# Rotated queries and new keys turned by VectorE blocks and a round trip through DRAM, instead of TensorE transposes

## The chip, the cores and the metric

The kernel runs on one NeuronCore of a Trainium2 chip. The metric is the device time of one execution in microseconds; several runs are taken and their median counts. Five engines work beside each other, each in the order in which its instructions were written out: TensorE (PE in the profile; its weight loads are shown as PEld), VectorE (DVE), ScalarE (ACT), GpSimd (POOL) and SyncE (SP, which here only issues DMAs). Where an instruction needs another engine's result it waits, and all that stands behind it on its own engine waits with it. DMAs are issued from SP's or GpSimd's queue and run on 16 DMA engines.

## The reference, cut to what matters

Four layers with residual sums work on `x` of 64 batches x 32 tokens x 512 channels, all in fp32. Layers 0 and 3 multiply by a 32x32 matrix chosen per batch, layer 1 is a linear layer with a low-rank adapter chosen per batch. Layer 2, where most of the time goes, is attention over a paged cache:

```python
q = jnp.einsum('bsd,ed->bse', x, Wq).reshape(bsz, seqlen, HQ, D)   # 32 heads of 128
k = ...Wk...reshape(bsz, seqlen, HK, D)                            # 8 heads
v = ...Wv...
q = _rope(_rmsnorm(q, q_norm_w), pos)
k = _rope(_rmsnorm(k, k_norm_w), pos)
k_all = concatenate([kc, k], axis=1)     # 512 cached keys by block_table, 32 new ones
scores = jnp.einsum('bqhd,bkhd->bhqk', q, k_all) * SCALE
probs = softmax(where(valid, scores, -1e30))
o = jnp.einsum('bhqk,bkhd->bqhd', probs, v_all)
return jnp.einsum('bse,de->bsd', o.reshape(bsz, seqlen, HQ * D), Wo)
```

`_rope` multiplies the normed vector by cosines, multiplies a copy with its halves swapped by sines, and adds the two. The part that concerns us is what happens to `q` and the new `k` between `_rope` and the scores: the projections leave them with tokens on the partitions, and the scores need them with the 128 head channels on the partitions.

## The kernel before, in words

Tokens are taken in 16 tiles of 128 (four batches of 32). Key heads come in two groups of four (`KG = 4`), and each key head serves four query heads (`REP = 4`). A *step* is one tile with one group, so there are 32 steps; two steps with the same group make a *pair* (16 pairs), whose projections share work in Strassen's manner. A *unit* is one batch in one group: four units a step, 128 in all. A *slot* is one key head of one unit, so there are 512 slots, and the loop `slot(i)` writes out, slot by slot, what every engine does; negative slots are the start, in which layer 1 runs and the first pair is projected. What is done in a slot beside the attention is entered in a plan by slot number (`at(slot, where, ...)`), and `where` ("fetch", "pool", "pe", "take", "late", "power", "turn", "dve", "keep", "act", "store") gives the place in the slot.

In slot i, TensorE computes the scores of head k of its unit (L848 and L851, against 544 keys in one two-bank tile `s_ps`, of which there is one), transposes the probabilities of slot i-2 (`flip`, L890) and multiplies those of slot i-3 by the values (L900). VectorE adds the mask and takes the maximum (L856), copies the turned probabilities out of PSUM (L892) and takes reciprocals; ScalarE does the exponential (L867) and the division (L873, L874). GpSimd gathers a chunk of cached values (L105, one a slot), makes the next unit's mask `pen` (L819, one a unit) and issues some DMAs. SP loads each unit's 16 pages of keys into `kT` (L804) with page numbers read from a table, two units' buffers in turn: unit u's are issued in slot 4(u-1).

Between these lies the next pair's projection, placed so that it ends three slots before the pair's first scores (`AHEAD = 1`): blocks KV, 0 and 1 of `begin_block`, each with seven products (`project`, L664) whose sums VectorE takes into `raw` (L676). A block of queries covers eight heads of both tiles, which come out as four sets of four heads; KV gives the new values, which are stored, and one set of four keys a tile. A `Norm` then handles one set of four heads, 512 elements a partition: ScalarE's squares (L720), GpSimd's power -1/2 (L725, L727), and on VectorE `scale` (L732), `straight` (L739), `swapped` in two halves (L751) and `sum` (L761). `norm_piece` puts these four pieces into slots in order, first come first served, where VectorE's count of pieces in the slot is under two (three in each fourth slot). After the sum, `turn` (L766) has TensorE transpose the four heads into PSUM, and `keep` (L778) has ScalarE copy them to `qT` or `kT_new`. ScalarE copies a unit's new keys beside its cached pages (`begin`, L835), and `scores` reads `qT` from its own tile.

Output tiles `oT` go to DRAM by `store` (L940), half of them on SP's queue and half on GpSimd's, until the last three steps. After the last slot comes the output projection (L1351) and layer 3.

Of the kernel before, what the change touches and what calls it, by code (L numbers as in the profile page):

```python
# [43 lines left out]
P = 128  # L44
# [4 lines left out]
D = 128  # L49
# [28 lines left out]
def resid_kernel(  # L78
# [139 lines left out]

    o_dram = [
# [7 lines left out]
    with ExitStack() as l2:  # L227
# [6 lines left out]
        front_pool = l2.enter_context(tc.tile_pool(name="front", bufs=1))  # L234
# [135 lines left out]
        def rotary(t):  # L370


            if t < 2:
                step = pair_of[0].steps[t]
                step.rot = {kind: rotary_tile(kind, t) for kind in "qk"}
            else:
                rot = start_pool.tile([P, 2, 2, D], F32, name="rot", bufs=2)
                rot_of[t] = {"q": rot[:, 0], "k": rot[:, 1]}
# [11 lines left out]
        def rotary_tile(kind, i):  # L390
            return proj_pool.tile([P, 2, D], F32, name=f"rot_{kind}{i}")
# [177 lines left out]
        class Step:  # L569


            def __init__(self, s):
                self.g, self.t = steps[s]
                self.qT, self.rot = {}, {}

        class Pair:
# [24 lines left out]
            def load_rotary(self, kind):  # L601
                for i, step in enumerate(self.steps):
                    step.rot[kind] = rotary_tile(kind, i)
# [35 lines left out]
        class Block:  # L639
# [17 lines left out]
            def project(self, i, c):  # L657
                x, half, w = self.ORDER[i]
                if c == 0 and i % 2 and self.slots[2 * i] in range(-11, -2):
# [12 lines left out]
            def new(self):  # L672
                return proj_pool.tile([P, REP, D], F32, name="raw", bufs=6)
# [6 lines left out]
            def take(self, i, norm):  # L680

                if i == 0:
                    self.u = self.new()
                    nc.scalar.copy(self.u, self.ps.rearrange("p (h d) -> p h d", h=REP))
                elif i == 1:
                    norm.raw = self.new()
                    self.add(norm.raw, self.u)
                elif i == 2:
                    self.add(self.u, self.u)
                elif i == 3:  # L690
                    self.v = self.new()
                    self.add(self.v, self.u)
                elif i == 4:
                    norm.raw = self.new()
                    self.add(norm.raw, self.v)
                elif i == 5:
                    self.add(self.v, self.v)
                    norm.raw = self.v
                    self.add(self.u, self.u)
                else:  # L700
                    self.add(self.u, self.u)
                    norm.raw = self.u

            def store_values(self, norm, i):
                step = self.pair.steps[i]
                nc.sync.dma_start(
                    out=vn_dram[step.g][step.t], in_=norm.raw.rearrange("p h d -> p (h d)")
                )

        class Norm:  # L710


            def __init__(self, pair, i, k=None):
                self.i, self.step, self.k = i, pair_of[pair].steps[i], k

            def squares(self):
                self.ss = small.tile([P, REP], F32, name="ss")
                sq = proj_pool.tile([P, D], F32, name="sq")
                for h in range(REP):
                    nc.scalar.activation(  # L720
                        sq, self.raw[:, h, :], AF.Square, accum_out=self.ss[:, h : h + 1]
                    )

            def power(self):
                nc.gpsimd.tensor_scalar(self.ss, self.ss, D * EPS, None, ALU.add)  # L725
                self.rstd = small.tile([P, REP], F32, name="rstd")
                nc.gpsimd.tensor_tensor(  # L727
                    self.rstd, self.ss, minus_half.to_broadcast([P, REP]), ALU.pow
                )

            def scale(self):
                nc.vector.tensor_tensor(  # L732
                    self.raw, self.raw, self.rstd.unsqueeze(2).to_broadcast([P, REP, D]), ALU.mult
                )

            def straight(self):
                kind = "k" if self.k is None else "q"
                self.a = proj_pool.tile([P, REP, D], F32, name="rot_a", bufs=2)
                nc.vector.tensor_tensor(  # L739
                    self.a,  # L740
                    self.raw,
                    self.step.rot[kind][:, 0, :].unsqueeze(1).to_broadcast([P, REP, D]),
                    ALU.mult,
                )

            def swapped(self):
                kind = "k" if self.k is None else "q"
                self.b = proj_pool.tile([P, REP, D], F32, name="rot_b")
                half = D // 2
                for i in (0, 1):  # L750
                    nc.vector.tensor_tensor(  # L751
                        self.b[:, :, i * half : (i + 1) * half],
                        self.raw[:, :, (1 - i) * half : (2 - i) * half],
                        self.step.rot[kind][:, 1, i * half : (i + 1) * half]
                        .unsqueeze(1)
                        .to_broadcast([P, REP, half]),
# [3 lines left out]
            def sum(self):  # L760
                nc.vector.tensor_tensor(self.a, self.a, self.b, ALU.add)  # L761

            def turn(self):
                self.tp = ps_t.tile([P, REP, P], F32, name="head_ps", tag="t")
                for h in range(REP):
                    nc.tensor.transpose(self.tp[:, h, :], self.a[:, h, :], ident)  # L766

            def keep(self):

                if self.k is None:  # L770
                    dst = front_pool.tile([P, NB, KG, S], F32, name="kT_new", bufs=3)
                    self.step.kT_new = dst
                else:
                    dst = front_pool.tile(
                        [P, NB, REP, S], F32, name=f"qT_{self.i}", bufs=(4, 6)[self.i]
                    )
                    self.step.qT[self.k] = dst
                nc.scalar.copy(  # L778
                    dst.rearrange("p j h s -> p h j s"),
                    self.tp.rearrange("p h (j s) -> p h j s", j=NB),  # L780
                )

        class Unit:


            def __init__(self, u):
# [6 lines left out]
                self.kT = room["kT"].tile([P, NPP + 1, KG, PSIZE], F32, name="kT")  # L793
# [38 lines left out]

            def begin(self):

                nc.scalar.copy(  # L835
                    self.kT[:, NPP].rearrange("p k s -> p (k s)"),
# [690 lines left out]
```

## Time and profile before

| | us |
|---|---|
| median of 3 runs (2440.8 to 2450.85) | 2444.19 |
| the profiled execution | 2442.28 |
| its span | 2440.4 |
| PE busy in the span | 2401.3 |
| DVE / ACT / POOL busy | 1658.7 / 1397.4 / 1163.8 |
| first scores start | 183.4 |
| DMA: MB moved, mean share of 16 engines | 459.18, 62.7% |

In a row of a group, the shape is followed by the count, then the busy time of the group in us and the mean length of one in ns, then the time its engine was idle before it and who ended that. PE's lengths overlap, since matmuls are pipelined: for what a group costs TensorE, the distance between starts counts. A row of the stretches has, after its window and length, each engine's busy time and count, the clock granted to TensorE as a share, the DMA engines' mean busy share and the rate in GB/s. In a row of a queue's time line, the start and the time from the first issue to the end of the last one come first. SP's rows of waits have the total, the number and the longest.

### The profile page before, as it was taken

What the parts mean: (1) busy time and instruction counts of PE and PEld (TensorE: products, weight loads), DVE (VectorE), ACT (ScalarE), POOL (GpSimd) and SP (SyncE); (2) the same over time, 40 slices, a digit from 0 to 9 for tenths busy, and PEclk for the clock granted to TensorE, in tenths of its full rate; (3) what the DMA queues carried; (4) which work ended last, traced back from release to release, by engine and by line L of the source; (5) the groups of instructions that cost most, each with busy time, mean ns of one, the idle gap of its engine ahead of it and who ended that gap; (6) DMA issues with size and microseconds to landing.
All of it is one profiled execution on the core that took longest, in us unless ns stands there. A gap on an engine that the chain in (4) does not pass through costs nothing.

```text
span 2440.4 us, 47152 instructions
## 1 busy us (share of the span) xinstructions
PE 2401.3 (98%) x13792; PEld 1866.5 (76%) x13792; DVE 1658.7 (68%) x3611; ACT 1397.4 (57%) x4005; POOL 1163.8 (48%) x1146
## 2 busy tenths in 40 slices
PE   7999999999999999999999999999999999999999
PEld 4557777777777777777777777777777788888887
DVE  5667778777777777787777777777777856333222
ACT  2246767777777777777777777777676754000000
POOL 3336555555555556655655555655555653000000
PEclk9999999999999999999999999999999999999999
DMA  8877666666767677866666666666667874333221
GB/s 270 281 241 204 192 195 197 191 204 189 208 186 212 185 218 231 248 189 199 176 190 178 193 171 195 176 189 179 192 183 225 258 242 157 107 117 123 87 91 57
DMA packets 458320, 459.18 MB, mean 188 GB/s; under 512 B 53008, under 2 KB 381072, under 8 KB 454480
## 3 DMA queue, kind: packets, MB, share of 16 engines
q1 hardware_dynamic: 402560, 276.03, 37.4%
q0 software_dynamic: 54928, 179.09, 24.7%
q8 instruction: 111, 1.82, 0.3%
q14 instruction: 145, 1.19, 0.2%
q10 hardware_dynamic: 576, 1.05, 0.1%
HBM read 384.66 MB, written 79.69 MB: 190 GB/s over the span
## 4 chain that ended last, share of the span: by engine, by line
PE 91%; DMA 3%; DVE 2%; issue 1%; ACT 1%; SPq 1%; POOL 0%; ACTq 0%; DVEq 0%; POOLq 0%
PE proj_ps L664 23%; PE o_ps L900 17%; PE out_ps L1351 15%; PE s_ps L848 10%; PE pT_ps L890 9%; PE s_ps L851 8%; PE head_ps L766 3%; PE l_ps L490 2%; PE o_ps L913 1%; DMA o<-oT 1%; DMA kT<-kT 1%; PE s_ps L883 1%; SPq L804 1%; PE mix_ps L1369 1%; DMA rot<-rot 1%
## 5 line engine op out<-in xcount | busy, mean ns | idle before, releaser
L105 POOL DMA_INDIRECT v_sb<-v,v_rows x512 | 544.9, 1064 | 364.1 <-PE o_ps L900 253.6
L900 PE MATMUL o_ps<-pT,v_sb 128*128 128x128 f32 x4096 | 624.0, 275 | 0.0
L900 PEld LDWEIGHTS o_ps<-pT,v_sb 128*128 128x128 f32 x4096 | 578.4, 191 | 27.2 <-DVE pT L892 0.5
L867 ACT ACTIVATE sm<-sm,top 128x544 f32<-128x544 f32 x512 | 380.9, 744 | 345.2 <-DVE top L856 340.7
L856 DVE CUSTOM_DVE_ANT_0 sm<-s_ps,pen 128x544 f32<-128x544 f32 x512 | 369.1, 721 | 114.5 <-PE s_ps L851 110.0
L873 ACT ACTIVATE sm<-sm,share 128x512 f32<-128x512 f32 x512 | 369.9, 722 | 101.0 <-DVE share L872 88.5
L892 DVE COPY pT<-pT_ps 128x512 f32<-128x512 f32 x512 | 353.0, 689 | 56.9 <-PE pT_ps L890 17.7
L848 PE MATMUL s_ps<-kT,qT 128*128 128x288 f32 x1024 | 334.4, 408 | 1.4 <-DMA kT<-kT 1.1
L890 PE MATMUL pT_ps<-ident,sm 128*128 128x128 f32 x2048 | 310.2, 274 | 4.2 <-ACT qT L778 2.7
L851 PE MATMUL s_ps<-kT,qT 128*128 128x256 f32 x1024 | 305.8, 380 | 4.2 <-issue 4.2
L676 DVE TENSOR_TENSOR raw<-proj_ps,raw 128x512 f32<-128x512 f32 x332 | 224.1, 687 | 121.2 <-PE proj_ps L664 121.1
L848 PEld LDWEIGHTS s_ps<-kT,qT 128*128 128x128 f32 x1024 | 179.4, 190 | 148.4 <-issue 126.9
L819 POOL TENSOR_SCALAR pen<-key_f,seq_f 128x544 f32<-128x544 f32 x128 | 284.1, 2220 | 12.9 <-DMA kT<-kT 1.6
L890 PEld LDWEIGHTS pT_ps<-ident,sm 128*128 128x128 f32 x2048 | 239.0, 141 | 8.4 <-ACT qT L778 4.4
L720 ACT ACTIVATE sq<-raw 128x128 f32<-128x128 f32 x640 | 198.5, 310 | 77.3 <-DVE raw L676 61.9
L851 PEld LDWEIGHTS s_ps<-kT,qT 128*128 128x128 f32 x1024 | 194.8, 190 | 58.7 <-issue 5.1
L105 POOL DMA_INDIRECT mix_rows<-in_w,cond_rows x32 | 36.8, 1149 | 353.3 <-DVE mix_diag L170 301.1
L725 POOL TENSOR_SCALAR ss<-ss 128x4 f32<-128x4 f32 x160 | 38.8, 243 | 348.0 <-ACT sq L720 344.4
L872 DVE RECIPROCAL share<-total 128x1 f32<-128x1 f32 x512 | 83.8, 164 | 177.0 <-ACT sm L867 162.8
L1401 ACT COPY p<-out_ps 128x256 f32<-128x256 f32 x7 | 2.6, 372 | 333.1 <-PE out_ps L1351 333.1
L664 PE MATMUL proj_ps<-sum,x 128*128 128x512 f32 x380 | 188.1, 597 | 0.4 <-DVE raw L676 0.4
L727 POOL TENSOR_TENSOR rstd<-ss,minus_half 128x4 f32<-128x4 f32 x160 | 167.6, 1047 | 13.3
(176 smaller groups left out, 3517.2 us busy)
## 6 DMA issues: line engine op xcount, KB each, us to landing
kT<-kT SPq DMA_DIRECT2D x2048, 64.0 KB
o_in<-o SPq DMA_DIRECT2D x28, 1024.0 KB
o<-oT POOLq DMA_DIRECT2D x69, 256.0 KB
o<-oT SPq DMA_DIRECT2D x58, 256.0 KB
page_rows<-in_kv_cache SPq DMA_DIRECT2D x32, 256.0 KB
v<-in_kv_cache SPq DMA_DIRECT2D x32, 256.0 KB
kT<-page_rows SPq DMA_DIRECT2D x32, 256.0 KB
vn<-raw SPq DMA_DIRECT2D x32, 256.0 KB
```

The costliest lines, as they stand in the source:

```text
L105: nc.gpsimd.indirect_dma_start(out=dst, out_offset=None, in_=table, in_offset=bass.IndirectOffsetOnAxis(ap=index, axis=0),)
L664: nc.tensor.matmul(self.ps, lhsT=self.pair.x[x][:, c if x == "b" else half.start + c, :], rhs=blocks(self.b)[w][:, c, :], start=(c == 0), ...
L819: nc.gpsimd.tensor_scalar(self.pen, key_f, seq_f[:, self.b : self.b + 1], BIG, ALU.is_ge, ALU.mult)
L848: nc.tensor.matmul(ps[:, first:HID], lhsT=q, rhs=self.kT[:, :n1, k, :], start=True, stop=True)
L851: nc.tensor.matmul(ps[:, HID : first + LA], lhsT=q, rhs=self.kT[:, n1:, k, :], start=True, stop=True)
L856: nc.vector.tensor_tensor_reduce(out=sm, in0=ps[:, first : first + LA], in1=self.pen, scale=1.0, scalar=3e38, op0=ALU.add, op1=ALU.min, ac ...
L867: nc.scalar.activation(sm, sm, AF.Exp, bias=top, scale=-1.0, accum_out=total)
L873: nc.scalar.activation(sm[:, :L], sm[:, :L], AF.Copy, scale=share)
L890: nc.tensor.transpose(ps[:, c, :], self.sm[k][:, c * P : (c + 1) * P], ident)
L892: nc.vector.tensor_copy(pT, ps)
L900: nc.tensor.matmul(o_of[self.s, k][:, self.j, :], lhsT=self.v[c][:, k * D : (k + 1) * D], rhs=self.pT[k][:, c, :], start=(self.j == 0 and ...
L1351: nc.tensor.matmul(ps[:, :HALF], lhsT=o[:, i, :], rhs=w[i // REP][:, i % REP, :], start=(i == 0), stop=(i == KG * REP - 1),)
```

## The change

The TensorE transposes of the heads and ScalarE's copies of them go. Norms are merged into doubles: one `Norm` now handles eight heads (both tiles' keys, or a tile's two sets of query heads in a block), 1024 elements a partition, so there are 80 instead of 160. Their sum moves from VectorE to GpSimd, one slot after `swapped`. Two slots after `swapped` at the earliest, VectorE turns the eight heads in blocks of 32x32 in one instruction, which puts, for each batch, 32 channels on the batch's 32 partitions. SP stores the result to a DRAM tile `qk` (one store for a tile's queries of a block, two for the keys; 16 x 6 = 96 stores of 256 or 512 KB), and for each unit GpSimd loads its new keys and its four heads of queries into the end of the unit's `kT` buffer, four slots ahead of its scores, with one DMA of 320 KB (128 of them), whose access pattern puts the 4 x 32 channels on 128 partitions. `scores` reads the queries from there.

With that, the projection starts eight slots earlier (`AHEAD = 9`, and the start of the kernel has eight slots more); `kT` has three buffers, each longer by four rows, and a unit's page loads are issued in slot 4(u-2)+1; the planner counts VectorE's pieces in microseconds up to `ROOM`; all output stores go to GpSimd's queue, and `oT` has four buffers instead of three. In the start, more of the projections' sums use the scores' PSUM tile.

```diff
+    qk_dram = [
+        [dram.tile([P, NC, (1 + KG) * P], F32, name=f"qk_{g}_{t}") for t in range(NT)]
+        for g in range(NG)
+    ]
...
             def scale(self):
+                raw = self.raw.rearrange("p i h d -> p (i h) d")
                 nc.vector.tensor_tensor(
-                    self.raw, self.raw, self.rstd.unsqueeze(2).to_broadcast([P, REP, D]), ALU.mult
-                )
+                    raw, raw, self.rstd.unsqueeze(2).to_broadcast([P, 2 * REP, D]), ALU.mult
+                )
...
             def sum(self):
-                nc.vector.tensor_tensor(self.a, self.a, self.b, ALU.add)
+                a, b = [x.rearrange("p i h d -> p (i h d)") for x in (self.a, self.b)]
+                nc.gpsimd.tensor_tensor(a, a, b, ALU.add)
 
             def turn(self):
-                self.tp = ps_t.tile([P, REP, P], F32, name="head_ps", tag="t")
-                for h in range(REP):
-                    nc.tensor.transpose(self.tp[:, h, :], self.a[:, h, :], ident)
-
-            def keep(self):
...
-                nc.scalar.copy(
-                    dst.rearrange("p j h s -> p h j s"),
-                    self.tp.rearrange("p h (j s) -> p h j s", j=NB),
-                )
+
+                self.turned = self.raw.rearrange("p i h d -> p (i h d)").rearrange(
+                    "p (c m s) -> p c m s", c=NC, s=S
+                )
+                nc.vector.transpose(
+                    self.turned, self.a.rearrange("p i h (c e) -> p c (i h) e", c=NC)
+                )
+
+            def store(self):
+                pair = self.block.pair
+                for i in (0, 1) if self.i == KV else (self.i,):
+                    step = pair.steps[i]
+                    if self.i == KV:
+                        heads, first, n = slice(i * REP, (i + 1) * REP), 0, P
+                    else:
+                        heads, first, n = slice(0, 2 * REP), (1 + 2 * self.block.b) * P, 2 * P
+                    nc.sync.dma_start(
+                        out=qk_dram[step.g][step.t][:, :, first : first + n],
+                        in_=self.turned[:, :, heads, :].rearrange("p c m s -> p c (m s)"),
+                    )
...
-                self.kT = room["kT"].tile([P, NPP + 1, KG, PSIZE], F32, name="kT")
+                self.kT = room["kT"].tile([P, NPP + 1 + KG, KG, PSIZE], F32, name="kT")
...
+            def fetch_heads(self):
+
+                nc.gpsimd.dma_start(
+                    out=self.kT[:, NPP:].rearrange("d n k s -> d (n k s)"),
+                    in_=qk_dram[self.g][self.t][self.j * S : (self.j + 1) * S].rearrange(
+                        "e c f -> c e f"
+                    ),
+                )
+
             def begin(self):
 
-                nc.scalar.copy(
-                    self.kT[:, NPP].rearrange("p k s -> p (k s)"),
-                    step_of[self.s].kT_new[:, self.j].rearrange("p k s -> p (k s)"),
-                )
...
-                q = step_of[self.s].qT[k][:, self.j].rearrange("p h s -> p (h s)")
+                q = self.kT[:, NPP + 1 + k].rearrange("p h s -> p (h s)")
...
-            queue = nc.sync if k < 2 and s < len(steps) - 3 else nc.gpsimd
-            queue.dma_start(
+            nc.gpsimd.dma_start(
...
+        ROOM = 2.0
+        COST = {"scale": 1.2, "straight": 1.2, "swapped": 1.3, "turn": 1.2}
+        NEXT = {"scale": "straight", "straight": "swapped", "swapped": "turn"}
...
+            for piece in pieces:
+                ready, norm, name = piece
+                if ready <= slot and busy.get(slot, 0) + COST[name] <= ROOM:
+                    break
+            else:
                 return
...
+            if name == "turn":
+                pieces.pop(at_piece)
+                at(slot + 1, "fetch", norm.store)
+                return
+            later = name == "swapped"
+            if later:
+                at(slot + 1, "take", norm.sum)
+            pieces[at_piece] = (slot + 2 * later, norm, NEXT[name])
...
-        AHEAD = 1
+        AHEAD = 9
...
-            at(KG * (u - 1) if u > 1 else ready + 3 * u, "fetch", make, unit_of, u, Unit, u)
+            at(KG * (u - 2) + 1 if u > 2 else ready + 3 * u, "fetch", make, unit_of, u, Unit, u)
...
+            at(KG * u - (4 if u else 3), "fetch", call, unit_of, u, "fetch_heads")
...
-                    room["kT"] = l2.enter_context(tc.tile_pool(name="kT", bufs=2))
+                    room["kT"] = l2.enter_context(tc.tile_pool(name="kT", bufs=3))
```

## The prediction

> **What bounds the kernel now.** I read the page first (engine shares, then the chain), then a table of stretches, then the groups by shape, then SP's queue. The profiled execution took 2442.28 us, 2440.4 of them span; it stands 1.9 under the median of the three runs, 2444.19, so a sum made on it is a sum on the median within 0.1%. A change under 0.5% (12 us) can't be told from none.
>
> ```profile
> PE 2401.3 (98%) x13792; PEld 1866.5 (76%) x13792; DVE 1658.7 (68%) x3611; ACT 1397.4 (57%) x4005; POOL 1163.8 (48%) x1146
> ...
> PE 91%; DMA 3%; DVE 2%; issue 1%; ACT 1%; SPq 1%; POOL 0%; ACTq 0%; DVEq 0%; POOLq 0%
> ```
>
> TensorE is the path. The stretches (PE, PEld, DVE, ACT, POOL busy; clock; DMA share; GB/s) say where nothing else ends a wait:
>
> ```profile
> 150.00:183.00 33.00, 30.04 (x116) 15.95 (x114) 21.95 (x44) 13.40 (x47) 10.21 (x16) 1.00 0.76 241
> ...
> 240.00:1900.00 1660.00, 1657.88 (x10093) 1274.85 (x10092) 1271.21 (x2825) 1200.75 (x3487) 961.35 (x924) 1.00 0.67 196
> ...
> 900.00:1000.00 100.00, 99.75 (x588) 76.50 (x587) 75.64 (x167) 72.07 (x213) 63.65 (x64) 1.00 0.81 247
> ...
> 1950.00:2000.00 50.00, 44.96 (x306) 39.80 (x305) 28.27 (x64) 28.46 (x69) 28.39 (x30) 0.97 0.78 248
> ```
>
> From 240 to 1900 us TensorE idles 2.1 us in all, so every microsecond of its work removed there is one off the end, until another queue takes over. One pair of steps (32 slots) takes 117.5 us there, and of these VectorE is busy 1271.21/1660 x 117.5 = 90.0, ScalarE 85.0, GpSimd 68.0.
>
> The removed turns in TensorE's order: four transposes of a head group start at 1011.87 and the scores start at 1012.31.
>
> ```profile
> 1011.87 0.60 PE L766 MATMUL head_ps<-ident,rot_a 128*128 128x128 f32 x4
> 1012.31 0.65 PE L848 MATMUL s_ps<-kT,qT 128*128 128x288 f32 x2
> ```
>
> So a group costs 0.44 us of TensorE, start to start, not the 0.60 that its pipelined ends show.
>
> **What goes.** 160 groups (640 transposes) x 0.44 = 70.4 us of TensorE: 10 groups, 4.4 us, a pair, so 117.5 becomes 113.1. With up to 0.45 a group it would be 72 at most; I take 70. ScalarE loses the copies out of these (160 x 0.57) and the key copies (128 x 0.293), 8.0 us a pair: 85 becomes 77. It was not the path; priced at 0.
>
> **VectorE**, per pair, from these rows:
>
> ```profile
> L761 DVE TENSOR_TENSOR rot_a<-rot_a,rot_b 128x512 f32<-128x512 f32 x160 | 119.8, 749 | 2.6
> ...
> L751 DVE TENSOR_TENSOR rot_b<-raw,rot_q 128x256 f32<-128x256 f32 x256 | 101.4, 437 | 0.0
> ...
> L628 DVE TENSOR_TENSOR sum<-wq,sum 128x1024 f32<-128x1024 f32 x8 | 9.7, 1212 | 0.0
> ```
>
> Ten sums go (-7.5). Scale and straight become 5 + 5 of 1024 elements at 1.21 for 10 + 10 of 512 at 0.69 (-1.7); swapped, 10 of 512 at 0.69 for 20 of 256 at 0.43 (-1.7). Five block transposes of 1024 come; the trace has none. Bounds: two PSUM copies of 512 at 0.689 (1.4) less nothing, and twice a 1024-element operation (2.4); I take 1.21, the row of equal size: +6.1. VectorE goes from 90.0 to 85 (91 at the upper end) of 113.1: it keeps over 20 us, and a slot's scores leave it about 1.5 us of lag (3.1 us slot less 0.9 of scores and 0.7 of maximum). Price 0; without that cover each transpose's excess would count, 75 x 1.2 = 90 us.
>
> **GpSimd.** Ten pairs of power operations (0.243 + 1.047) become five of 8 elements (pow 1.05 if fixed, 2.1 if by element): -12.9, +6.5 to 11.7. Eight head loads and four more output stores at 0.594 a direct issue (1.064 if they cost what a gather does) add 7.1 to 12.8. That makes 69 to 80, plus five sums X of 1024 elements. X is the unknown. Below: the same sum on VectorE, 2 x 0.68 = 1.4. Nearest row on the engine:
>
> ```profile
> L819 POOL TENSOR_SCALAR pen<-key_f,seq_f 128x544 f32<-128x544 f32 x128 | 284.1, 2220 | 12.9 <-DMA kT<-kT 1.6
> ...
> L727 POOL TENSOR_TENSOR rstd<-ss,minus_half 128x4 f32<-128x4 f32 x160 | 167.6, 1047 | 13.3
> ```
>
> 2.22 x 1024/544 = 4.2, twice that for two inputs, 8.4. I take 4.2 (same engine, streaming): 90 to 101 of 113, so it stays off the path. Its waits: a sum waits for VectorE's swapped, and the next value gathers queue behind it; the turn, two slots after swapped, waits for the sum. Two slots are 6.5 us and more, so at 4.2 neither is late. I add 2 us in all (0 to 30).
>
> Does the sum slow VectorE? A sum on VectorE that began while the mask ran on GpSimd took 1.10 instead of 0.67 us, and was not held until the mask's end at 1535.51:
>
> ```profile
> 1533.55 1.10 DVE L761 TENSOR_TENSOR rot_a<-rot_a,rot_b 128x512 f32<-128x512 f32 x1
> ...
> 1533.41 2.10 POOL L819 TENSOR_SCALAR pen<-key_f,seq_f 128x544 f32<-128x544 f32 x1
> ```
>
> At 0.43 more for each of 80 sums that is 34 us of VectorE beside TensorE, priced at 0. [...]
>
> **DMA.** Stores of 16 x 2.62 MB and loads of 128 x 0.328 MB are 83.9 MB on 459.18. At the page's own price (62.7% of the span for 459.18 MB) the loop's 0.67 becomes 0.67 x 117.5/113.1 + 0.12 = 0.81 to 0.82. The stretch 900:1000 ran at 0.81 and TensorE lost 0.25 us of 100. Price 0 to 10, inside the next term.
>
> **SP, and what waits behind it.** One pair period of SP from 563.25: eight groups of page loads and what lies between. Some of it:
>
> ```profile
> 563.25 10.18 SPq L804 DMA_DIRECT2D kT<-kT  x16
> 573.52 0.38 SPq L706 DMA_DIRECT2D vn<-raw  x1
> 573.95 0.58 SPq L826 DMA_DIRECT2D v_new<-vn  x1
> ...
> 575.29 0.55 SPq L292 DMA_DIRECT2D kT<-page_rows  x1
> ...
> 606.35 1.09 SPq L940 DMA_DIRECT2D o<-oT  x2
> ```
>
> The eight groups sum to 80.2, the others to 14, register loads of 0.6 to 1.1 before a group make about 7: 101 of 117.5. After: less 1.9 for the output stores, plus six stores at about 0.6: 103 of 113.1. SP is the fullest queue after TensorE. Each store waits for its turn on VectorE, with the next unit's page loads behind it; the head load waits on GpSimd for the store, with value gathers behind it; TensorE needs both. The last turn that a pair's first step needs comes 7 slots ahead of its scores, with a group of 16 page loads (10 us, 3 slots) between turn and store; then store and load, for which the chain lists landings of 2.2 (values) to 6.2 us (output). 10 + 2 x 4 + 1 of issues fits in 7 x 3.5 = 24.5 us with 5 over. Three kT buffers (two before) let SP start page loads 7 slots ahead instead of 4, a relief that can gain no more than the loop's 2.1 us of idle time. Late by 0 to 3 us a pair: 0 to 45 us, I take 12.
>
> **The ends.** Start: unit 0's queries must go through turn, store and load before the first scores. From the last squares that is about 2 + 2 + 4 (VectorE) + 4 (sum) + 1.2 + 4 + 4 = 21 us; the next pair's key and value projections, moved ahead by 8 slots, cover 14 x 0.86 = 12. Before, TensorE already lost 3.0 of 33 us there. +0 to 9, I take 4. Tail: the last 12 slots before the early products have no projection, where 4 had none. They last 2.3 us each, 9.4 a unit against SP's 11 to 12; three units lose 6 us less SP's lead. +0 to 10, I take 4; the stretch 1950:2000 shows the same loss of 5.
>
> **Sum**: 2442.3 - 70 + 2 + 12 + 4 + 4 = 2394; I state 2392, since the first term may be 72.
>
> **Rivals.**
> (a) SP sets the pace: slower. For: its rows of waits, in four periods (400 to 870 us):
>
> ```profile
> SPq L940 <- ACT oT L932: 27.0, 8, 4.7
> SPq L804 <- PE s_ps L851: 25.8, 17, 3.3
> ```
>
> A store that SP reaches before its data costs it 3.4 us. Five turns a pair at that price are 17 us: 103 + 17 = 120 a pair, 2.5 over 117.5, so 15 x 2.5 + 8 for the ends: 2490. It decides from 14.5 us of waits a pair. Against: with three buffers a late SP stops waiting, and the old output waits are gone.
> (b) GpSimd sets the pace: from X = (113.1 - 69)/5 = 8.8, or 6.6 with its dearer rows; no gain left from X = 7.5 to 9.7. At 8.4 with the middle of 74: 116 a pair, 2442 - 70 + 15 x 2.9 + 10 = 2426. Against: 8.4 takes both the mask's rate and a doubling.
> (c) Half the gain: head loads late by 3 us every pair, both ends at their bounds: 2442 - 70 + 45 + 19 = 2436.
> (d) Hidden anyway: it would need VectorE or ScalarE near 117 of 117.5; they have 90 and 85. All costs at 0 gives 2370.
>
> **How the numbers follow.** The forecast (2370 to 2412) 0.62; still better, under 2368, 0.03; (c) and (b) as priced, 2412 to 2456, 0.17, two thirds of it under 2432; (a), or (b) beyond its bound, above 2456, 0.18. Range 2368 to 2456 leaves 0.03 and 0.18 outside; the likeliest case's own is 2370 to 2412. Faster 0.77, same 0.05, slower 0.18.
>
> **What would show it.** A pair period of about 113 us and PE still over 99% busy from 240 to 1880; block transposes near 1.2 us; sums on GpSimd at 2 to 4.5; value gathers on GpSimd not waiting for head loads. Wrong if SP shows hardly a gap, if scores wait for kT, or values for gathers, by several us a pair.

## The result, and the profile after

The changed kernel takes 2791.26 us, the median of four runs (2783.17 to 2795.01), against 2442.86 for the kernel before beside it: a ratio of 1.1415, with a 95% interval of 1.1376 to 1.1454. The forecast was 2392, in a range of 2368 to 2456. The change makes the kernel 14% slower, and the profiled execution (2783.17, span 2781.3) is one of those four. The page, first busy times and then the shares of the chain of waits:

```profile
PE 2422.4 (87%) x13152; PEld 1849.2 (66%) x13152; DVE 1610.6 (58%) x3211; ACT 1300.2 (47%) x3717; POOL 1435.4 (52%) x1252
...
PE 51%; DMA 17%; issue 12%; SPq 8%; DVE 5%; ACT 4%; POOL 4%; POOLq 0%; DVEq 0%; ACTq 0%
```

TensorE had 98% of the span and 91% of the chain; it has 87% and 51%, and 25% of the chain is now DMA or SP's queue. The loop as one stretch (columns as before: PE, PEld, DVE, ACT, POOL busy; clock; DMA share; GB/s):

```profile
300.00:2250.00 1950.00, 1672.64 (x9519) 1259.20 (x9518) 1231.05 (x2485) 1115.75 (x3227) 1210.31 (x1033) 0.94 0.75 208
```

TensorE is idle for 277 of 1950 us, where before it was idle for 2 of 1660. Two things are missing that one would look for in a kernel 14% slower: no other engine is full (the next is VectorE, 63%), and the DMA engines are busier by only 0.08 of their time. Where the time went, with TensorE's busy and idle time added up in three parts of the span (us; "pairs" is the mean of the first fourteen, from the starts of their first scores):

| | before | after | difference |
|---|---|---|---|
| first scores at (TensorE idle until then) | 183.4 (21.8) | 217.5 (46.5) | +34.1 (+24.7) |
| first to last scores | 1862.1 | 2169.0 | +306.9 |
| of it TensorE idle | 12.0 | 307.1 | +295.1 |
| of it TensorE busy | 1850.2 | 1861.9 | +11.7 |
| last scores to the end | 394.8 | 394.9 | +0.1 |
| a pair | 117.3 | 136.7 | +19.4 |

So nearly all of the 341 us is idle time of TensorE in the loop, some 20 us a pair, plus a later start. TensorE's busy time did not shrink although 640 transposes are gone; the reason stands in the next view, five stretches of 5 us around one of the stalls:

```profile
600.00:605.00 5.00, 5.00 (x30) 3.73 (x28) 1.26 (x4) 1.93 (x5) 0.00 (x0) 1.00 0.40 117
605.00:610.00 5.00, 0.03 (x1) 0.00 (x0) 0.00 (x0) 0.00 (x0) 0.00 (x0) 1.00 0.47 148
610.00:615.00 5.00, 0.00 (x0) 0.00 (x0) 0.00 (x0) 0.00 (x0) 0.75 (x1) 0.51 0.58 183
615.00:620.00 5.00, 0.00 (x0) 0.00 (x0) 1.40 (x2) 0.00 (x0) 4.53 (x4) 0.50 0.71 151
620.00:625.00 5.00, 4.53 (x16) 3.09 (x17) 2.57 (x7) 3.36 (x13) 4.43 (x4) 0.63 0.88 206
```

All four engines stand still together for ten microseconds, and the granted clock, 1.00 before the stall, is down to 0.50 in 615 to 620 and 0.63 where TensorE starts again. A later kernel below with the same matmuls and a mean clock of 0.995 (g4_all) has 1957.3 us of busy TensorE up to the last scores, where this one, at 0.945 in the mean, has 170.9 + 1861.9 = 2032.8; some 75 us go with the lower clock.

The time line of that stall, with the idle time before an instruction and its releaser in brackets:

```profile
585.33 8.89 SPq L827 DMA_DIRECT2D kT<-kT  x9
...
586.15 1.23 DVE L789 STREAM_TRANSPOSE raw<-rot_a 128x1024 f32<-128x1024 f32 x1
...
598.60 9.38 SPq L827 DMA_DIRECT2D kT<-kT  x16
...
609.15 0.58 SPq L801 DMA_DIRECT2D qk<-raw  x1
...
614.14 0.75 POOL L858 DMA_DIRECT2D kT<-qk  x1 [23.93 <-DMA kT<-kT]
615.20 1.00 POOL L105 DMA_INDIRECT v_sb<-v,v_rows  x1 [0.31 <-issue]
616.22 2.34 POOL L782 TENSOR_TENSOR rot_a<-rot_a,rot_b 128x1024 f32<-128x1024 f32 x1
618.60 1.25 DVE L789 STREAM_TRANSPOSE raw<-rot_a 128x1024 f32<-128x1024 f32 x1 [17.12 <-POOL rot_a L782]
...
620.47 2.08 PE L672 MATMUL proj_ps<-wk,x 128*128 128x512 f32 x2 [15.44 <-DVE raw L684]
```

Read it downwards. VectorE turns a set of heads at 586. SP gets to the store of it only at 609, 23 us later, because it is still busy with page loads; it does not wait for the turn. The head load on GpSimd waits 23.93 us for that store. Behind the head load on GpSimd stand a value gather and the sum of another norm; behind the sum, on VectorE, a transpose; behind the transpose the additions of the projections; and for those waits TensorE. (The releaser printed at the head load, a page load, is only the landing that came last in the trace.) GpSimd reaches this head load 2.8 us after the turn's end (587.38) and then stands for 23.93 us. Such a wait comes once a pair, fourteen times between 300 and 2250 us, for 15.2 to 25.4 us. SP's own waits, full span, before and after:

```profile
SPq L804 <- DMA kT<-kT: 9.7, 16, 1.9
```

```profile
SPq L827 <- DMA kT<-kT: 259.9, 201, 4.3
...
SPq L607 <- DMA kT<-kT: 34.0, 13, 4.0
SPq L801 <- DMA kT<-kT: 31.7, 21, 4.5
SPq L827 <- DMA qk<-raw: 31.2, 18, 5.4
...
SPq L801 <- DVE raw L789: 8.3, 1, 8.3
```

In the trace SP's DMAs take turns on eight semaphores (336 or 337 on each), and by the rows above a DMA waits there until the eighth before it has landed. Before, all rows of this kind came to 13 us between 300 and 1900 us. Now they are some 358 us between 300 and 2250, 25 a pair. The last row is the wait that the prediction had feared, of a store for its turn: 8.3 us, once.

The landings themselves are longer. From each issue to the last of its semaphore counts, median and ninetieth percentile between 300 and 1900 us: page loads 2.65 and 3.90 before, 4.27 and 8.65 after; value gathers 4.30 and 5.54 before, 5.89 and 9.15 after; the new head loads 9.06 and 10.21. A page load issued 0.6 us before the head load of 614.14 landed in 1.7 us, one issued 0.8 us after it took 7.6. So the theory to test (A): the head load itself is slow, and slows all that is in flight with it. The trace's DMA packets say how. A head load is 64 packets of 5120 bytes; between 300 and 1900 us of the kernel after, at most five of them run at once for over 99% of the time (3.3 in the mean), and from the first to the last of a load 5.8 us pass. That four of the 16 DMA engines carry a load is the author's estimate from these packets; the trace does not number the engines. The load's pattern is "e c f -> c e f": the slowest dimension is `c`, which has four values.

### The profile page after: what moved, and what is told of

The parts are those of the page before. It is cut to its first block, busy times and chain, and to the rows that moved or that the text cites. A ratio compares the mean times of both kernels' runs of the same rounds, so it can differ in the third digit from the quotient of the medians.

```text
span 2781.3 us, 45999 instructions
## 1 busy us (share of the span) xinstructions
PE 2422.4 (87%) x13152; PEld 1849.2 (66%) x13152; DVE 1610.6 (58%) x3211; ACT 1300.2 (47%) x3717; POOL 1435.4 (52%) x1252
## 4 chain that ended last, share of the span: by engine, by line
PE 51%; DMA 17%; issue 12%; SPq 8%; DVE 5%; ACT 4%; POOL 4%; POOLq 0%; DVEq 0%; ACTq 0%
PE out_ps L1386 13%; PE proj_ps L672 12%; PE o_ps L928 8%; DMA kT<-kT 8%; PE s_ps L876 5%; SPq L827 5%; PE s_ps L879 4%; DMA v_sb<-v,v_rows 4%; PE pT_ps L918 4%; ACT sq L731 2%; POOL rot_a L782 2%; PE l_ps L498 2%; ACT sm L895 2%; SPq L819 2%; DVE raw L684 1%
## 5 line engine op out<-in xcount | busy, mean ns | idle before, releaser
L928 PE MATMUL o_ps<-pT,v_sb 128*128 128x128 f32 x4096 | 645.6, 280 | 82.6 <-DMA v_sb<-v,v_rows 82.3
L928 PEld LDWEIGHTS o_ps<-pT,v_sb 128*128 128x128 f32 x4096 | 594.1, 195 | 120.8 <-DMA v_sb<-v,v_rows 91.7
L876 PE MATMUL s_ps<-kT 128*128 128x288 f32 x1024 | 349.4, 424 | 54.8 <-DMA kT<-kT 18.1
L876 PEld LDWEIGHTS s_ps<-kT 128*128 128x128 f32 x1024 | 195.7, 198 | 291.3 <-issue 179.7
L879 PE MATMUL s_ps<-kT 128*128 128x256 f32 x1024 | 315.6, 391 | 8.6 <-DMA kT<-kT 6.4
L858 POOL DMA_DIRECT2D kT<-qk x128 | 98.5, 770 | 327.8 <-issue 193.5
L918 PEld LDWEIGHTS pT_ps<-ident,sm 128*128 128x128 f32 x2048 | 246.4, 144 | 2.0 <-ACT page_rows L286 1.9
L879 PEld LDWEIGHTS s_ps<-kT 128*128 128x128 f32 x1024 | 200.9, 197 | 70.4 <-issue 11.3
L789 DVE STREAM_TRANSPOSE raw<-rot_a 128x1024 f32<-128x1024 f32 x80 | 98.6, 1233 | 226.2 <-POOL rot_a L782 226.2
L672 PE MATMUL proj_ps<-wk,x 128*128 128x512 f32 x128 | 79.1, 728 | 157.0 <-DVE raw L684 157.0
L782 POOL TENSOR_TENSOR rot_a<-rot_a,rot_b 128x1024 f32<-128x1024 f32 x80 | 189.5, 2369 | 40.2 <-DVE rot_b L773 38.2
```

The costliest lines, as they stand in the source:

```text
L672: nc.tensor.matmul(self.ps, lhsT=self.pair.x[x][:, c if x == "b" else half.start + c, :], rhs=blocks(self.b)[w][:, c, :], start=(c == 0), ...
L876: nc.tensor.matmul(ps[:, first:HID], lhsT=q, rhs=self.kT[:, :n1, k, :], start=True, stop=True)
L879: nc.tensor.matmul(ps[:, HID : first + LA], lhsT=q, rhs=self.kT[:, n1 : NPP + 1, k, :], start=True, stop=True)
L918: nc.tensor.transpose(ps[:, c, :], self.sm[k][:, c * P : (c + 1) * P], ident)
L928: nc.tensor.matmul(o_of[self.s, k][:, self.j, :], lhsT=self.v[c][:, k * D : (k + 1) * D], rhs=self.pT[k][:, c, :], start=(self.j == 0 and ...
```

## The experiments

### The shape of the head load, the slack, or the sums

A time given with a ratio is the median of four executions; the others are single ones, beside which a difference of some 10 us shows nothing (the kernel before took 2438 to 2452 us beside them).

Rival theories were B, that SP simply has its work in the wrong order or too much of it (stores behind 16 page loads), and C, that the sums on GpSimd hold up VectorE. The first experiment changes the shape alone. If the transpose puts channel 4e+c where it put channel 32c+e, the 128 partitions of a head load are one run of DRAM rows, and every channel still arrives on the same partition:

```diff
-                    self.turned, self.a.rearrange("p i h (c e) -> p c (i h) e", c=NC)
+                    self.turned, self.a.rearrange("p i h (e c) -> p c (i h) e", c=NC)
...
-                        "e c f -> c e f"
+                        "e c f -> (e c) f"
```

> The kernel after, but the head load reads 128 consecutive rows (the block transpose puts feature 4e+c where it put 32c+e, so that the 128 partitions of a load are one run of rows in DRAM). Theory A, the head load's shape: as it stands its 64 packets of 5120 bytes run four at a time for 5.5 us, and everything issued meanwhile lands with it; spread over all 16 DMA engines a load's packets are over in under 2 us, the median landing of page loads falls from about 4.2 to under 3.2 us and p90 from 8.5 to under 5, SP's waits for its own earlier page loads from 260 to under 80 us, the once-a-pair wait of 15 to 25 us before the head load goes, and the time is 2380 to 2440. Theory B, SP's order and number of instructions (stores behind 16 page loads): landings may shrink, but the store stays 15 to 25 us late once a pair, time 2700 to 2790. Theory C, the sums on GpSimd: 2750 to 2800, the sums still 18 us late once a pair.

Measured: 2558.97 us beside 2438.15 for the kernel before, a ratio of 1.0483 (1.0458 to 1.0507). Of the 348 us lost, 232 are back by the order of two dimensions. The 64 packets of a load are now over in 2.2 us (6.9 at once in the mean, up to 16 for over 99% of the time), a head load lands in 5.14 us, page loads in 2.89 (5.05 at the ninetieth percentile), and SP hardly waits for its own loads:

```profile
SPq L827 <- DMA kT<-kT: 22.2, 38, 1.2
```

Theory A holds for two thirds. It missed the forecast of 2380 to 2440: the wait before the head load did not go, it shrank to 6 to 14 us in all pairs but the last; and the transpose, which now reads in steps of 16 bytes, costs more:

```profile
L789 DVE STREAM_TRANSPOSE raw<-rot_a x80: 1979/2034/2109, 123.6 to 2059.0; 128x1024 f32<-128x1024 f32 x80
```

Theory C was tried by putting the sums back on VectorE in the kernel after:

```diff
-                nc.gpsimd.tensor_tensor(a, a, b, ALU.add)
+                nc.vector.tensor_tensor(a, a, b, ALU.add)
```

> The kernel after with the 80 sums back on VectorE. Theory A (shape of the head load): the head load still stalls GpSimd and SP is still held by slow landings, 2760 to 2800. Theory B (SP's order): the same. Theory C (sums on GpSimd are what holds turns, additions and TensorE): the waits of turns for sums (226 us) go, 2450 to 2600.

Measured: 2800.23. Theory C falls. TensorE's waits for additions go, and come back as waits for values:

```profile
PE o_ps L928 <- DMA v_sb<-v,v_rows: 211.1, 53, 15.3
```

The third keeps the slow head load and gives all turns four slots more:

```diff
-        AHEAD = 9
+        AHEAD = 13
```

> The kernel after with the projections 13 slots ahead for 9, so four slots (14 us and more) of slack between the last turn a step needs and its scores. Theory A: SP has hardly a gap and sets the pace, slack is eaten in the first pairs, 2720 to 2800. Theory B in the form that the store is merely ordered too late: the wait of 15 to 25 us a pair shrinks by 14, 15 pairs by 14 is 210, time 2560 to 2620. Theory C: 2760 to 2800.

Measured: 2776.52, a pair 135.5 us. This is the run that separates A from B. The slack does what it should, waits of more than 4 us before a head load go from sixteen to ten and the longest from 25.4 to 9.2 us, and yet the time falls by only 15 us, little more than the runs of the kernel after differ by. TensorE now waits for the page loads:

```profile
PE s_ps L876 <- DMA kT<-kT: 68.6, 19, 9.5
PE s_ps L879 <- DMA kT<-kT: 36.0, 12, 7.5
```

```profile
SPq L827 <- DMA kT<-kT: 238.0, 188, 4.3
```

SP's waits for its own earlier DMAs are still there, 27 us a pair, and its other waits are down to 3. SP needs about 135 us for a pair's work with or without the slack, and a queue that is too slow by 20 us a pair can be given no slack. The stall at the head load in the kernel after was the place where SP's lateness showed, not its cause.

### What is left: the order on SP

With the shape mended, theory D says that the rest of the loop's loss is the order: 16 page loads stand on SP between the last turn that a pair's first step needs and its store. Theory E says it is VectorE's dearer transposes and the sums. Two ways of curing the order, slack and a swap, on the kernel of e1_spread:

```diff
-        AHEAD = 9
+        AHEAD = 13
```

> The kernel of e1_spread (2559) with the projections 13 slots ahead for 9. What is left there: the store that the first head load of a pair needs stands on SP behind 16 page loads (11 us) and is 7 to 13 us late once a pair, GpSimd waits with it, TensorE idles 8 us a pair; and 34 us later first scores. Theory D (this order is the rest of the loop's loss): four more slots cover it, no wait over 3 us before a head load, pairs of 115 to 117 for 123, time 2559 less 14 pairs by 7 is 2460, 2440 to 2480, first scores still at about 217. Theory E (transposes of 2.03 us on VectorE and sums on GpSimd are the rest): 2530 to 2560.

```diff
-            at(KG * (u - 2) + 1 if u > 2 else ready + 3 * u, "fetch", make, unit_of, u, Unit, u)
+            at(KG * (u - 2) + 3 if u > 2 else ready + 3 * u, "fetch", make, unit_of, u, Unit, u)
```

> The kernel of e1_spread with each unit's page loads issued two slots later (5 slots ahead of its scores for 7), so that the last store a pair needs at its first head load stands ahead of that slot's 16 page loads on SP. Theory D: the same as four more slots, 2440 to 2490, if page loads still land in time (10 us of issue and 4 of landing in 5 slots of 3.5). Theory E: 2530 to 2560.

Measured: 2458.43 with the slack and 2536.47 with the swap. With the slack the longest wait before a head load is 3.3 us, a pair takes 116.7 us for 123.5, and first scores stay at 216.2, nearly all as theory D has it. (VectorE gains too: scales held up by the sums, of which more at the end, cost 44 us in e1_spread and 12 here. What share that has was not tested.) The swap brought less than D said, and its time lies in E's range: a pair takes 121.2, head loads still wait 5 to 6 us in most pairs (15.5 and 18.2 in two), and TensorE now waits 37 us for values. Its trace shows that page loads are not all that makes a head load wait. One turn ends at 672.9 us, SP issues its store at 674.5, GpSimd reaches the head load at 674.9 and can issue it only at 680.66, when the store has landed. The store's landing alone outlasts the 2 us that GpSimd leaves between turn and load. The same swap in the kernel after, with its slow head loads:

> The kernel after, with its slow head loads, and only the page loads two slots later. If the shape of the head load is the main cause and the order the lesser one: SP is still held by landings of 8 us and sets the pace, 2700 to 2800. If the order alone were enough: under 2620.

Measured: 2829.17, 38 us more than the kernel after (the expectation's upper end was 2800). The order alone gains nothing.

The fourth of this set leaves the reordering of channels to the GpSimd sum, which writes into `raw` in steps of 32 elements, so that VectorE reads one run again:

```diff
-                a, b = [x.rearrange("p i h d -> p (i h d)") for x in (self.a, self.b)]
-                nc.gpsimd.tensor_tensor(a, a, b, ALU.add)
+                a, b = [x.rearrange("p i h (e c) -> p (i h) e c", c=NC) for x in (self.a, self.b)]
+                dst = self.raw.rearrange("p i h (c e) -> p (i h) e c", c=NC)
+                nc.gpsimd.tensor_tensor(dst, a, b, ALU.add)
...
-                    self.turned, self.a.rearrange("p i h (c e) -> p c (i h) e", c=NC)
+                    self.turned, self.raw.rearrange("p i h (c e) -> p c (i h) e", c=NC)
```

> As f2_spread_order, with the order of features changed in the GpSimd sum, which writes its 1024 elements in steps of 32, and no longer in VectorE's block transpose, which reads them in one run again: transposes back from 2.03 to 1.23 us, 4 us of VectorE a pair. The sum may cost more than 2.37 us, up to twice. Theory D: VectorE is off the path, 2430 to 2490, within 15 of f2_spread_order. Theory E: 40 to 60 less than f2_spread_order.

Measured: 2515.91, ratio 1.0268 (1.0251 to 1.0285), 20.6 less than f2_spread_order; between D's 15 and E's 40. The sum costs nothing more, the transpose is at its old price:

```profile
L783 POOL TENSOR_TENSOR raw<-rot_a,rot_b 128x1024 f32<-128x1024 f32 x80 | 192.6, 2407 | 23.3 <-DVE rot_b L773 21.3
...
L790 DVE STREAM_TRANSPOSE rot_a<-raw 128x1024 f32<-128x1024 f32 x80 | 98.5, 1231 | 35.9 <-POOL raw L783 35.7
```

### The start, and a version that beats both

At the start of f1_spread_ahead13 SP issues the page loads of three units in one run from 175 to 205 us; a turn that ends at 192.7 is stored at 207.0. Units 1 and 2 get their ordinary place:

```diff
-            at(KG * (u - 2) + 1 if u > 2 else ready + 3 * u, "fetch", make, unit_of, u, Unit, u)
+            at(KG * (u - 2) + 1 if u > 0 else ready, "fetch", make, unit_of, u, Unit, u)
```

> The kernel of f1_spread_ahead13 (2458) with the page loads of units 1 and 2 at their ordinary 7 slots ahead of their scores, no longer 3 and 6 slots behind unit 0's. At the start SP issues three units' page loads in one run from 175 to 205 us, and the store of a turn that ended at 192.7 goes out at 207. Theory F (this run of page loads is the start's loss): first scores at 195 to 203 for 216, time 2436 to 2446. Theory G (the chain of turn, store, load and its 0.6 us instructions is itself that long): first scores at 212 to 216, time 2450 to 2460.

Then the same with the reordering in the sum:

> g1_start with the order of features changed by the GpSimd sum in place of the transpose (transposes 1.23 us for 2.04, 4 us of VectorE a pair). In f1_spread_ahead13 TensorE idles 3.3 us a pair, mostly for additions and maxima of VectorE. With VectorE earlier: pairs of 114.5 for 116.5, 30 us less than g1_start, 2400 to 2420, faster than the kernel before by 1 to 2%. If VectorE is no cause of that idle time: within 8 of g1_start.

Measured: 2453.96 and 2429.95. In g1_start, first scores come at 208.9, not at 195 to 203: seven of the 34 us were this run of page loads, which makes theory F's cause real and a fifth of the later start. The total is 4.5 lower, less than single runs can tell. g4_all is at 0.9927 of the kernel before (0.9909 to 0.9946), 19 us or 0.7% faster: a pair takes 115.4 us for 117.3, and first scores are at 205.4, still 22 later than before. The forecast for it (2400 to 2420) was too good by ten: its pairs were to take 114.5. Its loop, in the stretch that the prediction showed of before:

```profile
240.00:1900.00 1660.00, 1627.55 (x9662) 1238.67 (x9660) 1248.19 (x2512) 1130.51 (x3280) 1189.23 (x1047) 1.00 0.80 246
```

The DMA engines are busy for 0.80 at 246 GB/s, more than in the kernel after (0.75, 208), and TensorE is idle for 2%. A mean share of 0.80 was no trouble here; head loads with 3.3 packets at once in the mean were, in the kernel after (TensorE idle for 14% at a share of 0.75).

### The shape by itself

The strictest test adds one DMA to g4_all and compares its two shapes: a second load of each unit's heads into a tile that nothing reads (the output buffers go from four to three for the room). The first kernel has the pattern shown, the second "e c f -> c e f" in its place, and they differ in nothing else.

```diff
+                if self.u == 0:
+                    return
+                nc.gpsimd.dma_start(
+                    out=room["attn"].tile([P, (1 + KG) * P], F32, name="extra", bufs=1),
+                    in_=qk_dram[self.g][self.t][self.j * S : (self.j + 1) * S].rearrange(
+                        "e c f -> (e c) f"
+                    ),
+                )
...
-                oT = room["attn"].tile([P, REP, P], F32, name="oT", bufs=4)
+                oT = room["attn"].tile([P, REP, P], F32, name="oT", bufs=3)
```

> The kernel of g4_all (2430) with a second load of each unit's heads, 320 KB into a tile that nothing reads, behind the first, as one run of 128 rows; the value output buffers are three for four to make room. 42 MB more at the same shape as the first load. Both theories of the head load (its shape, or its bytes and instructions): if the shape is what costs, this one costs little: 2430 to 2480; if bytes and instructions: 2550 or more.

> As h16_extra_spread, and the second load in the order of the kernel after (feature block first). Same bytes, same instructions, same tile. If the shape is what costs: its packets run four at a time again, page loads land at over 4 us in the median and SP waits for them, 2650 to 2850. If bytes and instructions: within 25 of h16_extra_spread.

Measured: 2473.43 in the first shape, 2891.71 in the second, 42 above the upper end of its forecast. The extra 42 MB in the good shape, with one output buffer fewer, cost 43 us; the same bytes and issues in the other shape cost 418 more. SP's queue in the one and in the other:

```profile
SPq L828 <- DMA kT<-kT: 31.4, 60, 1.6
```

```profile
SPq L828 <- DMA kT<-kT: 230.6, 179, 3.8
```

Page loads land in 3.59 us (5.75) in the one and 4.55 (9.11) in the other. So the order of two dimensions, and neither the bytes nor the number of DMAs, is the main cause. The order also changes the sequence of addresses in DRAM, which no run separates from the number of packets at once. In the kernel after the packets themselves are only a little longer than in e1_spread (0.30 against 0.25 us in the mean), while half as many run at once (3.3 against 6.9), so by the trace most of it is the number at once.

### What the sums on GpSimd are worth

> The kernel of g4_all (2430) with the five sums of a pair on VectorE in place of GpSimd, still writing in steps of 32. VectorE gets 5 operations of 1.2 us (2.0 if writing in steps costs what reading in steps cost the transpose) a pair: 6 to 10 us on 86 of 115. If VectorE's lag is what still idles TensorE: 1.5 to 3 us a pair, 2450 to 2480. If nothing of VectorE is on the path any more: 2420 to 2440.

In g4_all with `nc.vector` for `nc.gpsimd` in the sum: 2486.07, ratio 1.0186 (1.0167 to 1.0205), a pair 119.5 us, 56 us more than g4_all in all (each beside its own run of the kernel before, 47 us slower against 19 faster).

```profile
L783 DVE TENSOR_TENSOR raw<-rot_a,rot_b 128x1024 f32<-128x1024 f32 x80 | 162.0, 2025 | 0.0
...
PE s_ps L912 <- DVE top L885: 38.2, 66, 1.8
```

The sum takes 2.03 us there, where it writes in steps (1.29 in e2_sum_dve, where it does not); 10.1 us of sums a pair on VectorE make the pair 4.1 us longer. The time is beyond both cases of the expectation. With the loads mended, moving the sums to GpSimd is a good part of this change; in the kernel after itself it is worth no more than e2_sum_dve's 9 us.

## Why the prediction was wrong, point by point

**What goes: right.** TensorE's work in a pair is 113 us in g4_all (1627.55/1660 x 115.4), as the prediction had it. In the kernel after the gain exists, but some 75 us at a lower clock (0.945 in the mean, 0.995 in g4_all) take it back.

**VectorE: its size right, its price wrong.** The transposes take 1.23 us (1.21 taken), VectorE 86 us a pair (85). "Price 0" was not true: between g1_start and g4_all VectorE's busy time falls by 3.4 us a pair (90.1 to 86.7) and the pair by 1.6, in i1_sum_dve it rises by 7.3 (to 94.0) and the pair by 4.1. That is about half a microsecond of time for one of VectorE, with VectorE busy for 75% of a pair; the cover of 20 us is not a cover slot by slot. From the mask's row the prediction took 0.43 us a sum for what GpSimd costs VectorE, and priced it at 0; in the kernel after a scale beside a sum took up to 2.37 us for 1.21 (last section), and the scales lose 9 us in all to the sums and the mask. In the kernel after itself it does not matter, as SP is later.

**GpSimd: sizes right.** The sum takes 2.37 us, within 1.4 to 8.4 and under the 4.2 taken from the mask's rate. Powers of 8 take 1.69 us, head loads 0.77 an issue. The wait of 2 us a program (0 to 30) is the wrong term: the prediction looked at sums that wait, and not at sums behind a head load that waits.

**"SP, and what waits behind it": the step that failed.** It had 12 us (0 to 45) and is nearly all of the 295 of idle time. Three things in it were wrong. First, "store and load, for which the chain lists landings of 2.2 (values) to 6.2 us (output)", taken as 4 each: the store took 5.93 in the median and the head load 9.06, so 10 + 5.9 + 9.1 + 1 is 26 us, more than the 24.5 there were. Second, the prediction counted what a late head load does to those who need it, and not what its transfer does to every other one. Each of a pair's eight head loads delays the page loads in flight (the three issued 0.8 to 2.2 us after the load of 614.14 landed in 7.2 to 7.6 us; between 300 and 1900 us, page loads issued 0.5 to 3 us after a head load landed in 8.3 in the median, those from 9 us after one to 3 us before the next in 2.3), and since SP waits for the eighth DMA before the one that it issues, that is 25 us of waits a pair in a queue that had 10 to spare (105 us of work and 7 of other waits make up the rest of 137; the prediction had 103). Third, it held the chain against the scores, seven slots after the turn, though the head load stands four slots ahead of them and GpSimd, which runs ahead of TensorE, stops there. In the stall above GpSimd reached it 2.8 us after the turn's end, so that even with the 10 us of page loads and the landing of 4 that were forecast, the gathers and sums behind it would have stood for some 11 us (an estimate from these numbers). e1_spread, where the landings are short, still has 6 to 14 us of this, and four more slots take it away. The pattern stood in the diff. The trace of before even had its like: the `v_new` loads, 64 KB with a slowest dimension of four, land in 3.5 us in the median, against 2.65 for the page loads of the same size. (The two differ in more than that dimension, and no run shows why the head load's pattern keeps few packets in flight.)

**DMA share, 0 to 10 us: the wrong measure.** The share was 0.75 in the kernel after, under the forecast, because the program was slower. What counted here is how many packets of a head load run at once (3.3 in the mean, 6.9 in e1_spread), which the mean share does not show.

**The ends: start mis-sized, tail 0.** The first scores come 34 us later (forecast 4, bound 9), of which 25 are idle time of TensorE and 9 work moved ahead. The chain of turn, store, load was forecast at 21 us with landings of 4, and SP's run of three units' page loads was not in it (7 us of the 34, by g1_start); 22 us remain in g4_all, whose start was not taken apart further. The tail is 394.9 against 394.8.

**The rivals.** (a), SP sets the pace, is what happened, and its price of 2490 was too low by 300: it let SP wait for turns, which cost 8.3 us, not for landings. Its argument against, "with three buffers a late SP stops waiting", held for data and says nothing of SP's own DMAs. (b), GpSimd, was far off: busy for 62% of the loop. (c) had the late head loads, at 3 us a pair instead of some 20.

**Its own signs.** Of the signs that the prediction named, the lengths came true (transposes near 1.2, sums from 2 to 4.5) and the waits did not: SP shows hardly a gap, scores wait for `kT`, and value gathers wait behind head loads, which it had listed as what would make it wrong. The third `kT` buffer was not tried by itself.

## What to carry to other kernels

Before costing a DMA by its bytes, read its access patterns as written in the instruction: here a load of 320 KB with a slowest dimension of four had 3.3 packets at once in the mean, for 6.9 in the other order, and delayed what was in flight (page loads 4.27 us in the median, for 2.89), at a mean share of 0.75. Where one queue issues many small loads with a fixed number in flight, a longer landing is a slower queue: price it as (landing in time of trouble)/(loads in flight) per load against the issue time (here 8.65 / 8 = 1.1 us at the ninetieth percentile, against some 0.6), before looking for slack. Where a queue must wait for data, hold the chain against the place of the waiting instruction in its queue, and not against the last user of the data. When several engines stall together, follow the first wait to the queue that is late, and ask if it is late once (then slack helps, as in f1_spread_ahead13) or every period (then it does not, as in e3_ahead13).

## What the runs showed of the hardware

The prediction argued from one row that VectorE is not held until the end of a GpSimd instruction. With sums on GpSimd it is, sometimes. In f1_spread_ahead13 a scale of 1024 elements, two operands from SBUF, began in the middle of a sum:

```profile
186.72 2.34 POOL L782 TENSOR_TENSOR rot_a<-rot_a,rot_b 128x1024 f32<-128x1024 f32 x1
...
187.20 0.69 DVE L684 TENSOR_TENSOR raw<-s_ps,raw 128x512 f32<-128x512 f32 x1 [0.79 <-issue]
...
187.80 2.34 DVE L747 TENSOR_TENSOR raw<-raw,rstd 128x1024 f32<-128x1024 f32 x1
```

The scale takes 2.34 us instead of 1.21: it ends 1.08 after the sum's end at 189.06, as if it had done nothing until then. The addition before it, with one operand from PSUM, ran at its usual 0.69 inside the same sum. In the kernel after, a block sum of weights took 3.41 and 2.98 us for 1.20, each 1.09 after the end of the sum it fell into. So these VectorE operations with two operands from SBUF were held to the end of the sums, GpSimd operations with two inputs; in the kernel after, beside the mask, which has one streamed input and from which the prediction argued, a scale takes 1.2 to 1.65. (The two differ in more than their inputs; what makes the difference was not tested.) It costs little in the kernel after, where few two-operand instructions fall beside the sums: five scales between 300 and 1900 us. In e1_spread a scale that began 0.67 us before a sum, at 559.24, was held too: it took 4.12 us and ended 1.09 after the sum's end. There the scales take 44 us more in all than at 1.21 each.

VectorE's block transpose of 128x1024 fp32 takes 1.23 us in the kernel after, and 2.03 in e1_spread, where it reads in steps of four elements. A VectorE sum that writes in steps of 32 takes 2.03 as well (i1_sum_dve), for 1.29 (e2_sum_dve); GpSimd's takes 2.41 (f5_sum_permutes) for 2.37 (the kernel after): there the reordering costs 0.04 us a sum.
